# Reordering half-size sums, softmax additions and norm statistics on the vector engine, and splitting one output projection, in a two-layer attention kernel

## The chip, the cores and the metric

The kernel runs on one core of a Trainium2 chip. The metric is the device time of one execution in microseconds (us), lower being better. Engines are named as in the profile: PE (TensorE, with PEld for its weight loads), DVE (VectorE), ACT (ScalarE), POOL (GpSimd) and SP (SyncE, which here issues DMAs). "L633" is line 633 of the kernel before the change, unless the changed kernel is named.

## The reference

Eight images of 32 x 32 positions and 512 channels (1024 tokens each) pass through two attention layers, each with a group norm in front and a residual around it. All is float32.

```python
x = x + conv0(gn(x), w_qkv, w_proj, b_proj)      # gn: 32 groups, no scale or shift
x = x + conv1(gn(x), Wq, Wk, Wv, Wo, pos_emb_w, pos_emb_h)

def conv0(x, ...):                               # 16 heads of 32
    q, k, v = split_heads(x.reshape(B, 1024, 512) @ w_qkv)
    attn = softmax(q * 32 ** -0.5 @ k.T)
    return merge_heads(attn @ v) @ w_proj + b_proj

def conv1(x, ...):                               # 4 heads of 128
    q, k, v = x @ Wq * 128 ** -0.5, x @ Wk, x @ Wv
    scores = q @ k.T + relative_logits(q, pos_emb_w, pos_emb_h)
    return merge_heads(softmax(scores) @ v) @ Wo
```

## The kernel before, in words

**Projections.** Every 512 x 512 projection of 1024 tokens is done as two units (`u`), each with seven half-size products instead of eight, a Strassen-Winograd scheme. `seven` (L397) issues the products in the order 0, 5, 1, 4, 6, 2, 3 (`ORDER`). Products 0 and 1 read quarters of the input as they are. Products 4, 5, 6 and 2 read half-size sums, which `forming` (L339, additions L360, 128 x 1024 each) makes on DVE, in this order: s1 for product 4, s2 for product 5, a difference for product 6 and s4 for product 2. A product is a chain of matmuls L327 into one PSUM bank called x, y or z. Product 5 goes into y; then `a = y + p1` (L411) is formed on DVE, and product 4 continues in the same bank y, so that it cannot start before L411 has read y. `b = y + p1` (L419) does the same after product 4, and product 2 waits for it. The tile names carry the projection: `a_wo` belongs to the output projection of layer 1 (`after_1`), `y_wp` to that of layer 0 (`after_0`).

**Output projections.** Their results are added to the residual: on POOL (L502) from copies in SBUF, on DVE (L507, with bias L509) from PSUM. In layer 1 finished parts are transposed on DVE (L947) and stored through SP's queue. In layer 0 the statistics of the second norm are taken from the finished parts (`bn_stats` L259, `bn_aggr` L260).

**Norms.** `group_norm` takes averages on a 128 x 32 tile (`turned` L285 to `var` L296, eight small DVE instructions), a power on POOL (`rstd` L300), and then four scalings on DVE (L304, 128 x 1024 each).

**Layer-0 attention.** `attention_0` treats 4 heads at a time, in 64 steps per image (4 head groups, 2 halves of queries, 8 blocks of keys). A step makes a score tile `ps` (16 matmuls L603, 4 PSUM banks, one buffer), its exponential `e` (ACT L611, two buffers in SBUF), its share of the output `acc` (8 matmuls L622), and adds `e` to the running sum `es` on DVE (L631 for the first pair, L633 for the other six). After eight steps the sum goes through PE (`sums` L643) and is normalised on DVE and POOL. So the next `ps` waits for `e` to have read the last one, and `e` waits until DVE has added the `e` of two steps before.

**Passes and order.** The main loop runs nine passes. In pass b, layer-0 attention of image b is laid beside other work (`side_by_side`), in this order: output projection of layer 0 of image b-1 (`after_0`), output projection of layer 1 of image b-2 (`after_1`) woven with the second norm of image b-1 (`norm_1`), the three projections of layer 1 (`second`), attention of layer 1, and the first projections of image b+1 (`before_0`). The order on each engine is fixed when the kernel is built: by priorities that follow program order, and by `tc.issue_after(ins)`, which holds an instruction behind another in its engine's order. The variables `begun`, `half_done` and `added` hold the last L411, L419 and layer-1 addition for that purpose. Weights are streamed from HBM by SP, one 128 KB chunk to a product, in the order of a written `plan`.

In pass 1 `after_0` makes its four sums from layer-0's output before its products; in later passes the sums are made ahead, by a hook in the last projection (`forms_0`). After the last pass, `after_last` does the output projection of the last image with its products in two parts: `two_first` (0 and 1 of both units) and then `five_last`.

Of the kernel before, what the change touches and what calls it, by code (L numbers as in the profile page):

```python
# [27 lines left out]
def quick_path(  # L28
# [23 lines left out]
    nc = tc.nc  # L52
# [267 lines left out]

    added = [None]
# [17 lines left out]
    def forming(x, name, room=None, behind=None):  # L339


        a11, a12 = x[:, :HC, :NB], x[:, HC:, :NB]
        a21, a22 = x[:, :HC, NB:], x[:, HC:, NB:]
        if room is not None:
            s1, s2, s4 = [room[:, i, :].rearrange("p (c n) -> p c n", n=NB) for i in range(3)]
        else:
            s1, s2, s4 = [
                mem.tile([P, HC, NB], F32, tag=f"form{i}", name=f"f{i}_{name}", bufs=1)
                for i in (1, 2, 4)
            ]  # L350
        for op, out, one, other in (
            (nc.vector.tensor_add, s1, a21, a22),
            (nc.vector.tensor_sub, s2, s1, a11),
            (nc.vector.tensor_sub, a21, a11, a21),
            (nc.vector.tensor_sub, s4, a12, s2),
        ):

            late = behind() if behind is not None else None
            with tc.issue_after(late.ins) if late is not None else nullcontext():
                last_form[0] = op(out, one, other)  # L360
            yield 0
        return [a11, a12, s4, a22, s1, s2, a21]
# [34 lines left out]
    def seven(fs, u, rows, sink, name, hook=None):  # L397
# [13 lines left out]
        begun[0] = nc.vector.tensor_add(a, y, p1)  # L411
# [7 lines left out]
        half_done[0] = nc.vector.tensor_add(b, y, p1)  # L419
# [17 lines left out]
    def two_first(fs, u, sink, name):  # L437

        product = taken(fs, u, False)
        x = bank(f"x_{name}")  # L440
        product(x, 0, True)
        p1 = snapshot("e1", f"p1_{name}")
        nc.scalar.copy(p1, x)
        product(x, 1, False)
        sink.c11(x)
        return p1

    def five_last(fs, u, sink, name, p1):
        product = taken(fs, u, False)
        y = bank(f"y_{name}")  # L450
        product(y, 5, True)
        a = snapshot("es1", f"a_{name}")
        nc.vector.tensor_add(a, y, p1)
        sink.early(p1, a)
        product(y, 4, False)
        b = snapshot("es1", f"b_{name}")
        nc.vector.tensor_add(b, y, p1)
        sink.middle(b)
        z = bank(f"z_{name}")
        product(z, 6, True)  # L460
        p7 = snapshot("e1", f"p7_{name}")
        nc.scalar.copy(p7, z)
        product(y, 2, False)
        sink.c12(y, p1)
        product(z, 3, False)
        sink.c21(z, a)
        sink.c22(b, p7)

# [121 lines left out]
    def attention_0(q, k, v, b, blocks=range(NT)):  # L590
# [23 lines left out]
        def back(m, h, j, e):  # L614
# [14 lines left out]
            if j == blocks[1]:  # L629
                state["esum"] = mem.tile([P, HB, NB], F32, tag="es0", name=f"es_{name}", bufs=1)  # L630
                nc.vector.tensor_add(state["esum"], state["first"], e)  # L631
            elif j != blocks[0]:
                nc.vector.tensor_add(state["esum"], state["esum"], e)  # L633
# [153 lines left out]
    def load(b, st):  # L787
# [21 lines left out]
        st["xn"] = yield from forming(x, f"xn0_{b}", behind=lambda: added[0])  # L809
# [66 lines left out]
    def before_0(b, st, hook=None):  # L876
# [4 lines left out]
        yield from project_T(fs, WQ0, st["q"], f"q0_{b}")  # L881
# [9 lines left out]
    def after_0(b, st, hook=None):  # L891

        fs = st.pop("ao0") if "ao0" in st else forms(st["q0"], f"ao0_{b}", block(f"forms_{b}"))
        x = st["x1"] = block(f"x1T_{b}")
        xT = fetch(st["kept"], x)
        for u in range(2):
            bias = [bproj_sb[:, n * HC + u : n * HC + u + 1] for n in range(2)]
            stream.unit(WP, False, u)
            yield from seven(
                fs, u, False, Onto(halves(xT, u), bias), f"wp_{b}_{u}", hook if u else None  # L900
            )
            for n in range(2):
                statistics(st, xT, n * HC + u, f"1_{b}")

    def norm_1(b, st, after=None, behind=None):
        xT = chunks(st["x1"])
        st["kept"] = put_away(xT, f"1_{b}")
        yield from group_norm(st, xT, f"1_{b}", after, behind)

    def second(b, st):  # L910

        fs = forms(st.pop("x1"), f"xn1_{b}")
        q = st["ao"] = block(f"q1_{b}")
        yield from project_T(fs, WQ1, chunks(q), f"q1_{b}")
# [53 lines left out]
    def after_last(b, st):  # L968
# [4 lines left out]
        early = [x[:, :HC, :NB], x[:, HC:, :NB]]  # L973
        p1s = []
        for u in range(2):
            stream.unit(WO, False, u)
            p1s.append(two_first(early, u, sinks[u], f"wo_{b}_{u}"))
        fs = forms(x, f"ao1_{b}")
        for u in range(2):
            stream.unit(WO, False, u)  # L980
            five_last(fs, u, sinks[u], f"wo_{b}_{u}", p1s[u])
# [32 lines left out]

    def marked():
# [17 lines left out]

    FIRST = units(WQ0) + units(WK0) + units(WV0, True)
    plan = [(m, m is WV0, u, ORDER) for u in range(2) for m in (WV0, WQ0, WK0)]
    for b in range(B + 1):
        if b >= 1:
            plan += units(WP)
# [8 lines left out]
    plan += [(WO, False, u, some) for some in (FIRST_TWO, LAST_FIVE) for u in range(2)]  # L1047
# [24 lines left out]
    for b in range(B + 1):  # L1072
# [11 lines left out]
        if last is not None:  # L1084
            if past is not None:
                norm = norm_1(b - 1, last, after=lambda: half_done[0])
# [4 lines left out]
            if past is not None:  # L1091
                rest.append(woven(later(after_1, b - 2, past), norm, 3, 3))
# [22 lines left out]
        else:  # L1115
            rest.append(woven(rest_of_first(here), incoming, 0, 2))
# [505 lines left out]
```

## Time and profile before

| | us |
|---|---|
| median of 3 runs | 3848.02 (3847.01 to 3848.98) |
| profiled execution, its own time | 3848.35 |
| span of the profiled execution | 3846.6 |
| PE busy | 3789.4 (99%) |
| DVE busy | 2555.1 (66%) |
| ACT busy | 1760.2 (46%) |
| POOL busy | 621.6 (16%) |

The profile is of one execution. Busy time is the time in which an engine has an instruction at work; the rest of the span is its idle time, and a number in square brackets at an instruction in a timeline is the engine's idle time just before it, with what ended it. The granted clock (PEclk) is the share of full speed that TensorE was given, 0.998 as a mean over this execution. The profiled time is 0.33 us over the median, and 1.75 us over its span.

### The profile page before, as it was taken

To read this page: it belongs to the slowest core of one execution; us is meant where nothing else is said; L and a number is where in the kernel's file an instruction comes from. 1 tells how busy PE (TensorE), PEld (TensorE's weight loads), DVE (VectorE), ACT (ScalarE), POOL (GpSimd) and SP (SyncE) were. 2 spreads that over 40 slices of the span, in tenths; PEclk is the share of its full clock that TensorE was granted. 3 is DMA by queue.
4 is the path that set the end of the run, shared out by engine and by line. 5 is a ranking of instruction groups with operands and counts; after the bars stand their busy time and mean duration, and the time that the engine had idled before them with its cause. 6 is when DMAs were issued, how large, how long until landed. Compare 5 with 4: busy or idle time off the path is not lost.

```text
span 3846.6 us, 79883 instructions
## 1 busy us (share of the span) xinstructions
PE 3789.4 (99%) x34478; PEld 1376.3 (36%) x34478; DVE 2555.1 (66%) x2966; ACT 1760.2 (46%) x1830; POOL 621.6 (16%) x398
## 2 busy tenths in 40 slices
PE   9999999999999999999999999999999999999998
PEld 4222244222443234432343323433234332334353
DVE  6777775686755866558665686656866568665544
ACT  3554544545444454444544445444454445553132
POOL 1342101121011211012101121111210112001201
PEclk9999999999999999999999999999999999999999
DMA  6122120142202322023120241103311023110321
GB/s 185 61 88 81 41 59 6 44 122 62 56 9 83 89 54 56 13 92 85 45 55 16 93 93 38 50 21 98 90 40 41 26 96 78 33 37 31 109 41 26
DMA packets 482983, 234.72 MB, mean 61 GB/s; under 512 B 269600, under 2 KB 461376, under 8 KB 481600
## 3 DMA queue, kind: packets, MB, share of 16 engines
q1 hardware_dynamic: 470992, 213.74, 20.5%
q0 software_dynamic: 2608, 13.70, 1.0%
q8 instruction: 273, 4.47, 0.5%
q10 hardware_dynamic: 9024, 2.10, 0.3%
q14 instruction: 86, 0.70, 0.1%
HBM read 170.72 MB, written 58.72 MB: 60 GB/s over the span
## 4 chain that ended last, share of the span: by engine, by line
PE 88%; DVE 7%; ACT 2%; issue 2%; DMA 0%; SPq 0%; POOL 0%; DVEq 0%; ACTq 0%; POOLq 0%
PE ps L603 12%; PE ps L718 11%; PE acc L730 11%; PE acc L622 11%; PE y_q L327 4%; PE y_v L327 4%; PE y_k L327 4%; PE ps L719 3%; PE x_q L327 3%; PE x_v L327 3%; PE z_k L327 3%; PE x_k L327 3%; PE z_q L327 3%; PE z_v L327 3%; DVE es L633 2%; ACT e L611 2%
## 5 line engine op out<-in xcount | busy, mean ns | idle before, releaser
L611 ACT ACTIVATE e<-ps 128x2048 f32<-128x2048 f32 x512 | 961.7, 1878 | 840.1 <-PE ps L603 630.0
L633 DVE TENSOR_TENSOR es<-es,e 128x2048 f32<-128x2048 f32 x384 | 894.8, 2330 | 403.7 <-ACT e L611 400.4
L603 PE MATMUL ps<-q,k 32*64 32x512 f32 x8192 | 579.1, 614 | 17.1 <-ACT e L611 17.1
L622 PE MATMUL acc<-e,v 128*32 128x512 f32 x4096 | 546.7, 605 | 0.0
L721 ACT ACTIVATE e<-ps 128x512 f32<-128x512 f32 x512 | 305.7, 597 | 507.1 <-PE ps L719 436.4
L718 PE MATMUL ps<-q,k 128*128 128x512 f32 x1024 | 525.0, 594 | 0.2 <-DVE posT L704 0.2
L730 PE MATMUL acc<-e,v 128*128 128x512 f32 x1024 | 522.0, 593 | 0.3 <-ACT e L721 0.3
L588 POOL TENSOR_TENSOR q<-q,su 128x512 f32<-128x512 f32 x128 | 212.7, 1662 | 1550.3 <-DVE su L584 1427.7
L741 DVE TENSOR_TENSOR es<-es,e 128x512 f32<-128x512 f32 x384 | 290.4, 756 | 251.0 <-ACT e L721 248.4
L719 PE MATMUL ps<-posT,sel 128*128 128x512 f32 x512 | 406.6, 794 | 0.0
L718 PEld LDWEIGHTS ps<-q,k 128*128 128x128 f32 x1024 | 192.5, 190 | 230.1 <-issue 218.5
L603 PEld LDWEIGHTS ps<-q,k 32*64 32x64 f32 x8192 | 120.6, 130 | 410.1 <-issue 223.5
L730 PEld LDWEIGHTS acc<-e,v 128*128 128x128 f32 x1024 | 193.1, 189 | 147.3 <-issue 92.6
L622 PEld LDWEIGHTS acc<-e,v 128*32 128x32 f32 x4096 | 81.3, 108 | 412.7 <-issue 366.1
L631 DVE TENSOR_TENSOR es<-e,e 128x2048 f32<-128x2048 f32 x64 | 171.6, 2681 | 32.8 <-ACT e L611 32.7
L568 DVE STREAM_TRANSPOSE tu<-su 128x512 f32<-128x512 f32 x128 | 90.5, 707 | 97.3 <-ACT su L566 95.7
L719 PEld LDWEIGHTS ps<-posT,sel 128*128 128x128 f32 x512 | 97.3, 190 | 122.5 <-issue 122.5
L566 ACT COPY su<-sums 128x512 f32<-128x512 f32 x128 | 74.9, 585 | 131.2 <-PE sums L643 81.5
L704 DVE TENSOR_TENSOR posT<-pp,posT 32x512 fp32r<-32x512 f32 x128 | 112.0, 875 | 31.9 <-ACT posT L699 30.6
L492 POOL TENSOR_TENSOR k<-b_k,p_k 128x512 f32<-128x512 f32 x32 | 52.0, 1624 | 483.4 <-ACT p_k L425 472.7
L699 ACT CAST posT<-pp 32x512 fp32r<-32x512 f32 x128 | 105.9, 827 | 45.8 <-PE pp L686 44.7
L492 POOL TENSOR_TENSOR v<-b_v,p_v 128x512 f32<-128x512 f32 x32 | 51.6, 1614 | 433.9 <-ACT p_v L425 433.9
(214 smaller groups left out, 4546.0 us busy)
## 6 DMA issues: line engine op xcount, KB each, us to landing
w_qkv<-ws_qkv SPq DMA_DIRECT2D x168, 128.0 KB, 2.5
d<-x0T SPq DMA_DIRECT2D x32, 512.0 KB, 3.0
x1T<-d SPq DMA_DIRECT2D x32, 512.0 KB, 5.9
d<-x1T SPq DMA_DIRECT2D x32, 512.0 KB, 3.6
x2T<-d SPq DMA_DIRECT2D x32, 512.0 KB, 6.1
w_qkv<-in_L_conv_w_qkv SPq DMA_DIRECT2D x126, 128.0 KB, 2.2
out<-ot SPq DMA_DIRECT2D x240, 64.0 KB, 2.0
xs<-in_x SPq DMA_DIRECT2D x224, 64.0 KB, 2.5
```

The source lines that it names most:

```text
L327: ins = nc.tensor.matmul(out[columns, :], weights[:, columns], moving, start=start, stop=stop, skip_group_check=open_sum,)
L588: nc.gpsimd.tensor_tensor(dst, dst, su, op=ALU.mult)
L603: nc.tensor.matmul(ps[some, r, :], k[m][rows, j * P + 64 * i : j * P + 64 * i + 64], q[m][rows, h * NB : (h + 1) * NB], start=True, stop=True,
L611: nc.scalar.activation(e, ps, AF.Exp, scale=D0 ** -0.5)
L622: nc.tensor.matmul(acc[r * D0 : (r + 1) * D0, :], v[:, j, c0 : c0 + D0], e[:, r, :], start=(j == blocks[0]), stop=(j == blocks[-1]),)
L631: nc.vector.tensor_add(state["esum"], state["first"], e)
L633: nc.vector.tensor_add(state["esum"], state["esum"], e)
L718: nc.tensor.matmul(ps, k[h][:, keys], q[:, h, queries], start=True, stop=False)
L719: nc.tensor.matmul(ps, sel_flat[:, keys], posT[:, h, queries], start=False, stop=True)
L721: nc.scalar.activation(e, ps, AF.Exp, scale=1.0 / math.sqrt(D1))
L730: nc.tensor.matmul(acc, v[:, j, h * D1 : (h + 1) * D1], e, start=(j == 0), stop=(j == NT - 1),)
L741: added[0] = nc.vector.tensor_add(state["esum"], state["esum"], e)
```

## The change

Four things change, all of them in the order of instructions; the instructions themselves and the bytes moved stay the same.

- **Sums of a norm in two parts.** In the passes 2 to 6 (`sums_1`) the first two sums for layer 1's first projection are made at the end of the norm, each behind the latest layer-0 addition; the third and fourth come later, between products of that projection. For image 1 (`before_0` in pass 0) the fourth sum comes between products of its first projection.
- **Additions behind readers.** While the norm runs beside layer 1's output projection (`with_norm`), each layer-0 addition (L631, L633) is held behind the latest L411 or L419 (`reader`). The four scalings L304 are held behind the latest such addition (`summed`), and are woven in at other places (gap 14 at the places 0, 3, 6, 8 and 9 instead of gap 3). On DVE this gives, in the passes 2 to 6: `a_wo` of the first unit ahead of the addition that stood before it, the third L633 ahead of the scalings, the scalings in two pairs with an addition between them, `a_wo` and `b_wo` of the second unit each ahead of an addition. In pass 7 the order changes likewise, with other steps.
- **First output projection in two parts.** In pass 1 `after_0` goes through the new `in_two_parts`: products 0 and 1 of both units first, with the four sums beside them, then the five others. `after_last` uses the same function. The weights are streamed in that order.
- **Last statistics.** In pass 8 the last statistics (`look`) come behind the L411 of layer 1's output projection.

```diff
@@ -320,2 +320,6 @@
+    reader = [None]
+    summed = [None]
+    beside_norm = [False]
+
     added = [None]
@@ -338,3 +342,3 @@
-    def forming(x, name, room=None, behind=None):
+    def forming(x, name, room=None, behind=None, into=None):
@@ -350,3 +354,6 @@
             ]
-        for op, out, one, other in (
+        fs = [a11, a12, s4, a22, s1, s2, a21]
+        if into is not None:
+            into.extend(fs)
+        for i, (op, out, one, other) in enumerate((
             (nc.vector.tensor_add, s1, a21, a22),
@@ -355,5 +362,7 @@
             (nc.vector.tensor_sub, s4, a12, s2),
-        ):
+        )):
-            late = behind() if behind is not None else None
+            late = None
+            if behind is not None:
+                late = behind[i]() if isinstance(behind, tuple) else behind()
             with tc.issue_after(late.ins) if late is not None else nullcontext():
@@ -361,3 +370,3 @@
             yield 0
-        return [a11, a12, s4, a22, s1, s2, a21]
+        return fs
@@ -410,3 +419,3 @@
         a = snapshot("es1", f"a_{name}")
-        begun[0] = nc.vector.tensor_add(a, y, p1)
+        reader[0] = begun[0] = nc.vector.tensor_add(a, y, p1)
         sink.early(p1, a)
@@ -418,3 +427,3 @@
         b = snapshot("es1", f"b_{name}")
-        half_done[0] = nc.vector.tensor_add(b, y, p1)
+        reader[0] = half_done[0] = nc.vector.tensor_add(b, y, p1)
         sink.middle(b)
@@ -443,4 +452,6 @@
         nc.scalar.copy(p1, x)
+        yield HC
         product(x, 1, False)
         sink.c11(x)
+        yield HC
         return p1
@@ -452,8 +463,10 @@
         a = snapshot("es1", f"a_{name}")
-        nc.vector.tensor_add(a, y, p1)
+        begun[0] = nc.vector.tensor_add(a, y, p1)
         sink.early(p1, a)
+        yield HC
         product(y, 4, False)
         b = snapshot("es1", f"b_{name}")
-        nc.vector.tensor_add(b, y, p1)
+        half_done[0] = nc.vector.tensor_add(b, y, p1)
         sink.middle(b)
+        yield HC
         z = bank(f"z_{name}")
@@ -462,4 +475,6 @@
         nc.scalar.copy(p7, z)
+        yield HC
         product(y, 2, False)
         sink.c12(y, p1)
+        yield HC
         product(z, 3, False)
@@ -467,2 +482,22 @@
         sink.c22(b, p7)
+        yield HC
+
+    def in_two_parts(x, m, sinks, name, room=None, done=lambda u: None, behind=None):
+
+        early = [x[:, :HC, :NB], x[:, HC:, :NB]]
+        p1s, fs = [], []
+
+        def products():
+            for u in range(2):
+                stream.unit(m, False, u)
+                p1s.append((yield from two_first(early, u, sinks[u], f"{name}_{u}")))
+
+        def sums():
+            fs.extend((yield from forming(x, name, room, behind)))
+
+        yield from woven(products(), sums(), 0, 1)
+        for u in range(2):
+            stream.unit(m, False, u)
+            yield from five_last(fs, u, sinks[u], f"{name}_{u}", p1s[u])
+            done(u)
@@ -630,5 +665,9 @@
                 state["esum"] = mem.tile([P, HB, NB], F32, tag="es0", name=f"es_{name}", bufs=1)
-                nc.vector.tensor_add(state["esum"], state["first"], e)
+                other = state["first"]
             elif j != blocks[0]:
-                nc.vector.tensor_add(state["esum"], state["esum"], e)
+                other = state["esum"]
+            if j != blocks[0]:
+
+                with tc.issue_after(reader[0].ins) if beside_norm[0] else nullcontext():
+                    summed[0] = nc.vector.tensor_add(state["esum"], other, e)
             if j != blocks[-1]:
@@ -808,3 +847,12 @@
         yield from group_norm(st, xT, f"0_{b}")
-        st["xn"] = yield from forming(x, f"xn0_{b}", behind=lambda: added[0])
+        if b > 1:
+            st["xn"] = yield from forming(x, f"xn0_{b}", behind=lambda: added[0])
+            return
+        fs = st["xn"] = []
+        done, read = lambda: summed[0], lambda: half_done[0]
+        sums = st["sums0"] = forming(x, f"xn0_{b}", behind=(done, read, read, done), into=fs)
+        yield next(sums)
+        yield 0
+        for _ in range(2):
+            yield next(sums)
@@ -880,3 +928,5 @@
         st["q"] = chunks(st["q0"])
-        yield from project_T(fs, WQ0, st["q"], f"q0_{b}")
+        yield from woven(
+            project_T(fs, WQ0, st["q"], f"q0_{b}"), st.pop("sums0", iter(())), 0, 2 * len(ORDER)
+        )
         st["k"] = chunks(block(f"k0_{b}"))
@@ -892,13 +942,29 @@
-        fs = st.pop("ao0") if "ao0" in st else forms(st["q0"], f"ao0_{b}", block(f"forms_{b}"))
         x = st["x1"] = block(f"x1T_{b}")
         xT = fetch(st["kept"], x)
+        sinks = [
+            Onto(halves(xT, u), [bproj_sb[:, n * HC + u : n * HC + u + 1] for n in range(2)])
+            for u in range(2)
+        ]
+
+        def done(u):
+            def look(u=u):
+                for n in range(2):
+                    statistics(st, xT, n * HC + u, f"1_{b}")
+
+            if b == B - 1 and u:
+                st["look"] = look
+            else:
+                look()
+
+        if "ao0" not in st:
+            yield from in_two_parts(
+                st["q0"], WP, sinks, f"wp_{b}", block(f"forms_{b}"), done, lambda: summed[0]
+            )
+            return
+        fs = st.pop("ao0")
         for u in range(2):
-            bias = [bproj_sb[:, n * HC + u : n * HC + u + 1] for n in range(2)]
             stream.unit(WP, False, u)
-            yield from seven(
-                fs, u, False, Onto(halves(xT, u), bias), f"wp_{b}_{u}", hook if u else None
-            )
-            for n in range(2):
-                statistics(st, xT, n * HC + u, f"1_{b}")
+            yield from seven(fs, u, False, sinks[u], f"wp_{b}_{u}", hook if u else None)
+            done(u)
@@ -906,2 +972,6 @@
         xT = chunks(st["x1"])
+        if "look" in st:
+
+            with tc.issue_after(begun[0].ins):
+                st.pop("look")()
         st["kept"] = put_away(xT, f"1_{b}")
@@ -909,7 +979,20 @@
+    def sums_1(b, st):
+
+        fs = st["xn1"] = []
+        done = lambda: summed[0]
+        sums = st["sums1"] = forming(
+            st.pop("x1"), f"xn1_{b}", behind=(done, done, done, lambda: half_done[0]), into=fs
+        )
+        for _ in range(2):
+            yield next(sums)
+
     def second(b, st):
-        fs = forms(st.pop("x1"), f"xn1_{b}")
+        if "xn1" in st:
+            fs, sums = st.pop("xn1"), st.pop("sums1")
+        else:
+            fs, sums = forms(st.pop("x1"), f"xn1_{b}"), iter(())
         q = st["ao"] = block(f"q1_{b}")
-        yield from project_T(fs, WQ1, chunks(q), f"q1_{b}")
+        yield from woven(project_T(fs, WQ1, chunks(q), f"q1_{b}"), sums, 0, 2 * len(ORDER), (0, 3))
         posT = block(f"posT_{b}", dtype=F32R)
@@ -972,11 +1055,3 @@
         sinks = [Onto(halves(xT, u), then=put_out(b, st, xT, u)) for u in range(2)]
-        early = [x[:, :HC, :NB], x[:, HC:, :NB]]
-        p1s = []
-        for u in range(2):
-            stream.unit(WO, False, u)
-            p1s.append(two_first(early, u, sinks[u], f"wo_{b}_{u}"))
-        fs = forms(x, f"ao1_{b}")
-        for u in range(2):
-            stream.unit(WO, False, u)
-            five_last(fs, u, sinks[u], f"wo_{b}_{u}", p1s[u])
+        run(in_two_parts(x, WO, sinks, f"wo_{b}"))
@@ -1014,2 +1089,7 @@
+    def with_norm(part):
+        beside_norm[0] = True
+        yield from part
+        beside_norm[0] = False
+
     def marked():
@@ -1033,2 +1113,5 @@
+    def in_parts(m):
+        return [(m, False, u, some) for some in (FIRST_TWO, LAST_FIVE) for u in range(2)]
+
     FIRST = units(WQ0) + units(WK0) + units(WV0, True)
@@ -1037,3 +1120,3 @@
         if b >= 1:
-            plan += units(WP)
+            plan += units(WP) if b > 1 else in_parts(WP)
         if b == 1:
@@ -1046,3 +1129,3 @@
             plan += FIRST if b else units(WQ0) + units(WK0)[:1] + units(WV0, True)
-    plan += [(WO, False, u, some) for some in (FIRST_TWO, LAST_FIVE) for u in range(2)]
+    plan += in_parts(WO)
@@ -1085,3 +1168,7 @@
             if past is not None:
-                norm = norm_1(b - 1, last, after=lambda: half_done[0])
+                norm = norm_1(
+                    b - 1, last, after=lambda: half_done[0], behind=lambda: summed[0]
+                )
+                if coming is not None:
+                    norm = chain(norm, later(sums_1, b - 1, last))
             else:
@@ -1091,3 +1178,3 @@
             if past is not None:
-                rest.append(woven(later(after_1, b - 2, past), norm, 3, 3))
+                rest.append(with_norm(woven(later(after_1, b - 2, past), norm, 3, 14, (0, 3, 6, 8, 9))))
                 total += PRODUCT
@@ -1115,3 +1202,3 @@
         else:
-            rest.append(woven(rest_of_first(here), incoming, 0, 2))
+            rest.append(woven(rest_of_first(here), incoming, 0, 1))
             total += PRODUCT
```

## The prediction

> **What bounds the kernel now.** I read the page's busy line first, then the waits of PE, then the timeline around each wait. Times below are us from the span's start in the profiled execution.
>
> ```profile
> PE 3789.4 (99%) x34478; PEld 1376.3 (36%) x34478; DVE 2555.1 (66%) x2966; ACT 1760.2 (46%) x1830; POOL 621.6 (16%) x398
> ```
>
> PE is busy for 3789.4 of 3846.6, so it bounds the kernel, and the change leaves its instructions alone. What can be gained is its idle time, 57.2, and time lost at a reduced clock. The largest lines of PE's waits (total, times, longest):
>
> ```profile
> PE ps L603 <- ACT e L611: 17.1, 16, 2.9
> PE y_wo L327 <- DVE a_wo L411: 9.1, 6, 1.8
> PE sums L643 <- DVE es L633: 3.1, 2, 1.8
> PE y_wp L327 <- DVE forms L360: 2.5, 1, 2.5
> ```
>
> They are short and many. ACT is only 46% busy, so a wait for ACT's `e` usually means that ACT was itself held up. The timeline of pass 2, at the norm beside layer 1's output projection, shows by what:
>
> ```profile
> 843.11 2.98 DVE L304 TENSOR_SCALAR x1T<-x1T,back,rstd 128x1024 f32<-128x1024 f32 x4 [1.20 <-POOL rstd L300]
> 846.01 2.29 DVE L633 TENSOR_TENSOR es<-es,e 128x2048 f32<-128x2048 f32 x1
> 848.38 1.88 ACT L611 ACTIVATE e<-ps 128x2048 f32<-128x2048 f32 x1 [5.25 <-DVE es L633]
> 850.32 1.12 PE L603 MATMUL ps<-q,k 32*64 32x512 f32 x16 [0.98 <-ACT e L611]
> ...
> 854.02 4.64 DVE L633 TENSOR_TENSOR es<-es,e 128x2048 f32<-128x2048 f32 x2
> 858.59 0.68 DVE L411 TENSOR_TENSOR a_wo<-y_wo,p_wo 128x512 f32<-128x512 f32 x1
> 859.32 1.92 PE L327 MATMUL y_wo<-f_ao,w_o 128*32 128x512 f32 x16 [1.42 <-DVE a_wo L411]
> ```
>
> Two stalls, both by DVE's order. The addition at 846.01 stands behind four scalings, ACT's `e` waits for it (848.38), and PE for ACT: 0.98. Later `a_wo` stands behind two additions, and PE waits 1.42 to go on in the bank `y_wo`. The same pair recurs in passes 3 to 6 with the same figures, except 1.77 for the second in pass 4. DVE is idle for 1.20 just before the scalings: it lacks order there, not capacity.
>
> **The change part by part.**
>
> *Passes 2 to 6.* With the new order I replayed DVE, ACT and PE by the durations above. The third addition comes behind `var` (L296, done at 841.92): it needs an `e` that was done at 839.44, so it runs from 841.9 to 844.2. ACT's next `e` then waits only for its `ps` (matmuls at 845.51 to 846.62) and is done at 848.6; PE wants it at 849.34, behind 16 matmuls of x_wo. The 0.98 goes, with 0.7 to spare. `a_wo` of the second unit, ahead of its addition, is done near 855.4; PE wants y_wo at 856.7. So 1.42 goes, with 1.3 to spare. Gain: 5 x 0.98 + 4 x 1.42 + 1.77 = 12.35.
> What stands behind the moved work: the first addition (L631) now waits behind `a_wo` of the first unit, which waits for PE's y_wo (done 830.9). L631 runs from 831.8 to 834.0 instead of 831.1 to 833.35; `e` behind it ends at 836.0, and PE's next `ps` is due at 836.28: 0.3 to spare, the thinnest place of the change. The second pair of scalings and the two later sums are off the path: I place the fourth sum at 881.7, and product 2 of the next projection wants it at 885.5. Without that cover a late sum would cost 1.2 to 2.3 (L360 at 1.22 to 2.29 in this trace) per pass. SP gets one store a place earlier (`out` of the first part); its loads keep their order there, and POOL's order is unchanged.
>
> A rule speaks against putting the addition there. The Trainium skill, "GPSIMD Engine Reference", section 1 (Specifications), says that GpSimd's SBUF interfaces are shared with VectorE and that it contends with DVE instructions that have two SBUF inputs. The moved L633 is one, and POOL's `rstd` (1.02 at 842.06), which now runs with DVE idle, falls beside it. The trace agrees on contention: POOL's L502 took 3.34 beside an addition at 835.70, 1.28 alone at 839.17. By the rows as they stand, `rstd` is done at 843.1, and the first scalings start behind the addition, at 844.2. Stretched by 3.34/1.28, `rstd` ends at 844.7. The scalings' first pair (1.5) and the addition behind it then end near 848.6 instead of 848.1, and `e` wants that only after 850.4. By both the sum is 12.35; the rule takes only slack.
>
> *First output projection, pass 1.*
>
> ```profile
> 322.96 1.07 PE L603 MATMUL ps<-q,k 32*64 32x512 f32 x2 [1.04 <-ACT e L611]
> ...
> 325.25 1.23 DVE L360 TENSOR_TENSOR forms<-forms,q 128x1024 f32<-128x1024 f32 x1
> 326.53 2.94 PE L327 MATMUL y_wp<-forms,w_p 128*32 128x512 f32 x16 [2.50 <-DVE forms L360]
> 329.40 1.72 PE L603 MATMUL ps<-q,k 32*64 32x512 f32 x14
> ...
> core 0: us, PE busy (x) PEld busy (x) DVE busy (x) ACT busy (x) POOL busy (x), PEclk, DMA share, GB/s
> 325.00:330.00 5.00, 3.47 (x23) 0.83 (x30) 4.19 (x5) 0.00 (x0) 0.00 (x0) 0.73 0.91 362
> ```
>
> Product 5 waits 2.50 for the second sum, and then the granted clock is 0.73 over 325 to 330: 16 matmuls took 2.94 where 1.90 is usual (340.28), and 14 of L603 1.72 where 16 take 1.11. That is 1.04 + 0.61 = 1.65 more. With products 0 and 1 of both units first, 32 matmuls that need no sum fill the gap, and the 1.04 at 322.96 lies under them too: 1.04 + 2.50 + 1.65 = 5.2. Against it: L631 now stands behind three sums and so holds ACT's third `e`; by replay that stalls `ps` for about 0.9 in all. Net 4.3. Here a rule gives another figure. The Trainium skill, "TensorE: Matmul & The Clock Gate", section "Why this matters for your kernels", asks for no idle gaps over about 3 us, one idle window bringing the half clock. By it the 2.50 would not have cost the clock: 5.2 - 1.65 = 3.55, net 2.65. The trace differs: a gap of 2.50 here and one of 1.82 before 165.60 (clock 0.69 over 165 to 170) were each followed by it, one of 2.92 before 141.17 was not. I go by the row, 4.3; ends 2.6 and 5.2.
> POOL's additions and SP's weight chunks are reordered only here; no chunk is wanted before it was, in its new place, and the chunks land 2.2 to 2.5 after issue. A late one would show as PE waiting for DMA; I take 0, with up to 2.5 in the range.
>
> *Fourth sum of image 1, pass 0.*
>
> ```profile
> 134.94 2.00 DVE L360 TENSOR_TENSOR f_xn<-x0T,f_xn 128x1024 f32<-128x1024 f32 x1
> 136.87 2.28 DVE L631 TENSOR_TENSOR es<-e,e 128x2048 f32<-128x2048 f32 x1
> 139.24 1.88 ACT L611 ACTIVATE e<-ps 128x2048 f32<-128x2048 f32 x1 [5.47 <-DVE es L631]
> 141.17 1.12 PE L603 MATMUL ps<-q,k 32*64 32x512 f32 x16 [2.92 <-ACT e L611]
> ```
>
> The sum leaves its place before L631, which then starts 1.95 earlier: 1.95 of the 2.92 goes. The sum comes back two additions later, where DVE has 1.32 idle before 148.05; product 2 wants it near 155. If it pushes the slow additions at 156.08 (9.38 for two, beside POOL's L152), the stall of 1.82 there grows, at worst taking the 1.95 back. I take 1.95; ends 0 and 5.4 (1.95 + 1.82 + 1.65, should that stall and its clock go too).
>
> *Last statistics, pass 8.* `a_wo` at 3575.18 stood behind three L259 and an L260, and PE waited 1.62 for it, to 3575.90. With the statistics behind it, I take 1.4; ends 0.8 and 1.62.
>
> *Pass 7.* A wait of 1.31 (sums behind an addition, 3214.35) goes, but `a_wo` ahead of L631 there holds the next `e`: about 0.9 is lost again. Net 0.4; ends -1 and 1.3. *After the last pass* the order of PE and DVE is the same: 0.
>
> Sum: 12.35 + 4.3 + 1.95 + 1.4 + 0.4 = 20.4, so 3848.35 - 20.4 = 3827.95 against the profiled execution; the median is 0.33 lower. I say 3828. Stalls at 239.98 (1.53), 376.1 (1.85), 269.8 (1.14) and at the start (8.3 with the wait for x) stay, their order being unchanged.
>
> **The rivals.**
> *Waits move on (3836).* Additions held behind L411 and L419 make `e` late one step further on. For it: the 0.3 to spare at 836.28, and DVE is 82% busy in this stretch (4.89 of 6.00 over 842 to 848). Against it: the other spare times are 0.7 to 1.8. If one stall as large as the first, 0.98, plus 0.6 at the thin place, comes back in each of the five passes, 5 x 1.6 = 8 of the 20.4 is lost.
> *Only the single places gain (3840.7).* The scheduler's order holds but DVE's instructions stretch beside POOL (L633 2.54 at 835.36 against 2.29), and the loop keeps its stalls: 12.35 and the 0.4 drop out, 7.65 stays: 3848.35 - 7.65 = 3840.7.
> *Slower (3869).* One mechanism: at the thin place, L631 behind `a_wo` of the first unit. If L631 is more than 0.3 late, PE stalls there for the rest; from about 1.8 the half clock follows, as before 165.60, and the price is 1.8 + 1.65 = 3.45. At both units of six passes that is 12 x 3.45 = 41.4, against a gain of 20.4: 21 slower. It decides from 2.35 per place (28.2 in all: the gain and 7.7 more). The stall of 1.8 needs y_wo, and so L631, 2.1 later than by the replay. Nothing in the trace shows that.
> *It does not do what it says.* Were the orders as before where the stalls are, 3848. The order of the built kernel is as described, so this is small.
>
> **How the numbers follow.** Forecast as worked out, 3823 to 3833: 0.62. Waits move on, 3833 to 3840: 0.22. Only single places, 3840 to 3845: 0.07. No change: 0.04. Slower: 0.03. Better than 3823, with the stall of 165.60 and its clock gone: 0.02. The range 3822 to 3840 holds the first two and some of the last, 0.85; it is wider than the first case since the spare times are thin. Faster by over 0.2% (7.7, about what a measurement of this kernel tells from no change) means below 3840.3: 0.88; within 0.2%: 0.09; slower: 0.03.
>
> **What would show it.** In the profile after, PE's wait for `a_wo` L411 should fall from 9.1 to about 1, that for `forms` from 2.5 to near 0, and that for `e` from 17.1 to about 11. DVE's busy time should stay within a few us of 2555. The clock should be 1.00 at 325 to 330. The forecast is wrong if the waits for `e` keep or exceed 17, or a new line stands in the waits of PE: for the sums L360, for DMA of `w_p`, or for L419.

## The result, and the profile after

The changed kernel takes 3832.17 us (median of 6 runs, 3830.98 to 3833.13) against 3847.34 for the kernel before (median of 6, 3846.50 to 3848.98): 15.2 us less, ratio 0.996 with a 95% interval of 0.9947 to 0.9973. The profiled execution took 3830.98 (span 3829.2), 17.4 less than the one before.

The page's busy line of the changed kernel:

```profile
PE 3786.5 (99%) x34478; PEld 1377.4 (36%) x34478; DVE 2562.9 (67%) x2966; ACT 1761.1 (46%) x1830; POOL 653.4 (17%) x398
```

PE was busy for 2.9 less and the span is 17.4 shorter, so 14.5 of it is idle time of PE that went (57.2 to 42.7). The 2.9 less of busy time, with the same number of matmuls, is mostly time at the half clock: the profile before had two stretches with a granted clock of 0.5 (3.41 each, from 166.87 and from 327.30) between its start and its end, the one after had none. POOL is busy for 32 more with the same 398 instructions, since the additions that are held now run beside them (622.8 again in no_held below, where they are not held); the last section comes back to it.

The waits of PE after (total, times, longest). L420 is L411 of before, L428 is L419, L646 is L611, L672 is L631 and L633, L638 is L603; L464 is `a` in `five_last`:

```profile
PE ps L638 <- ACT e L646: 13.4, 16, 1.8
PE y_wp L331 <- DVE a_wp L464: 2.6, 2, 1.8
PE y_wo L331 <- DVE a_wo L420: 0.7, 1, 0.7
PE y_k L331 <- DVE b_k L428: 0.4, 1, 0.4
```

The wait for `a_wo` fell from 9.1 to 0.7, and the waits for `forms` (2.5) and for `es` (3.1) are off the list. The wait for `e` fell from 17.1 to 13.4 only, and there are new ones: `y_wp` for `a_wp`, and a small one, `y_k` for `b_k`. A wait for L419 was one of the forecast's signs of being wrong. The timeline of pass 2 shows what became of the loop's two stalls:

```profile
825.68 1.28 POOL L623 TENSOR_TENSOR q<-q,su 128x512 f32<-128x512 f32 x1 [11.55 <-DVE su L619]
826.03 3.07 DVE L672 TENSOR_TENSOR es<-e,e 128x2048 f32<-128x2048 f32 x1
...
829.22 1.88 ACT L646 ACTIVATE e<-ps 128x2048 f32<-128x2048 f32 x1 [5.05 <-DVE es L672]
...
831.15 1.12 PE L638 MATMUL ps<-q,k 32*64 32x512 f32 x16 [0.44 <-ACT e L646]
...
836.28 2.28 DVE L672 TENSOR_TENSOR es<-es,e 128x2048 f32<-128x2048 f32 x1
836.81 2.63 POOL L300 TENSOR_TENSOR rstd<-var,neg_half 128x4 f32<-128x4 f32 x1 [1.85 <-DVE var L296]
...
839.48 1.53 DVE L304 TENSOR_SCALAR x1T<-x1T,back,rstd 128x1024 f32<-128x1024 f32 x2 [0.31 <-POOL rstd L300]
...
849.75 0.68 DVE L420 TENSOR_TENSOR a_wo<-y_wo,p_wo 128x512 f32<-128x512 f32 x1
...
851.54 1.90 PE L331 MATMUL y_wo<-f_ao,w_o 128*32 128x512 f32 x16
```

The addition at 836.28 now stands ahead of the scalings, which come in pairs; `a_wo` at 849.75 is done 1.1 before PE takes y_wo up again at 851.54, with no wait in brackets. Both old stalls are gone. A small one is left at 831.15: the first addition, behind `a_wo`, took 3.07. It starts while POOL's instruction of 825.68 is at work; in the kernel before it started 0.22 ahead of the same instruction, and took 2.25 while POOL took 3.17:

```profile
831.10 2.25 DVE L631 TENSOR_TENSOR es<-e,e 128x2048 f32<-128x2048 f32 x1
831.32 3.17 POOL L588 TENSOR_TENSOR q<-q,su 128x512 f32<-128x512 f32 x1 [11.55 <-DVE su L584]
```

Where the 17.4 came from, by the start of the same exponential in both traces (the gain at the end of a stretch less that at its begin):

| stretch | forecast | in the profiles |
|---|---|---|
| pass 0, the sums of image 1 | 1.95 | 3.97 |
| pass 1, the first output projection | 4.3 | 1.75 |
| passes 2 to 6, five norms | 12.35 | 11.16 |
| pass 7 | 0.4 | 0.03 |
| pass 8 and the end | 1.4 | 0.5 |

### The profile page after: what moved, and what is told of

Same layout as the page of the kernel before. It is cut to its first block, busy times and chain, and to the rows that moved or that the text cites. A ratio compares the mean times of both kernels' runs of the same rounds, so it can differ in the third digit from the quotient of the medians.

```text
span 3829.2 us, 79905 instructions
## 1 busy us (share of the span) xinstructions
PE 3786.5 (99%) x34478; PEld 1377.4 (36%) x34478; DVE 2562.9 (67%) x2966; ACT 1761.1 (46%) x1830; POOL 653.4 (17%) x398
## 4 chain that ended last, share of the span: by engine, by line
PE 91%; DVE 5%; ACT 2%; issue 1%; DMA 0%; POOL 0%; DVEq 0%; SPq 0%; ACTq 0%; POOLq 0%
PE ps L638 13%; PE acc L657 12%; PE ps L757 11%; PE acc L769 11%; PE y_q L331 4%; PE y_v L331 4%; PE y_k L331 4%; PE ps L758 3%; PE x_q L331 3%; PE x_v L331 3%; PE z_k L331 3%; PE z_q L331 3%; PE x_k L331 3%; PE z_v L331 3%; DVE es L672 2%; ACT e L646 2%
## 5 line engine op out<-in xcount | busy, mean ns | idle before, releaser
L646 ACT ACTIVATE e<-ps 128x2048 f32<-128x2048 f32 x512 | 961.8, 1879 | 821.3 <-PE ps L638 637.9
L672 DVE TENSOR_TENSOR es<-es,e 128x2048 f32<-128x2048 f32 x384 | 890.8, 2320 | 386.6 <-ACT e L646 384.1
L638 PE MATMUL ps<-q,k 32*64 32x512 f32 x8192 | 577.8, 613 | 13.4 <-ACT e L646 13.4
L623 POOL TENSOR_TENSOR q<-q,su 128x512 f32<-128x512 f32 x128 | 201.7, 1575 | 1527.5 <-DVE su L619 1402.6
L638 PEld LDWEIGHTS ps<-q,k 32*64 32x64 f32 x8192 | 120.4, 129 | 405.5 <-issue 212.7
L672 DVE TENSOR_TENSOR es<-e,e 128x2048 f32<-128x2048 f32 x64 | 176.5, 2758 | 31.4 <-ACT e L646 31.3
L603 DVE STREAM_TRANSPOSE tu<-su 128x512 f32<-128x512 f32 x128 | 90.6, 708 | 97.3 <-ACT su L601 95.7
```

The source lines that it names most:

```text
L623: nc.gpsimd.tensor_tensor(dst, dst, su, op=ALU.mult)
L638: nc.tensor.matmul(ps[some, r, :], k[m][rows, j * P + 64 * i : j * P + 64 * i + 64], q[m][rows, h * NB : (h + 1) * NB], start=True, stop=True,
L646: nc.scalar.activation(e, ps, AF.Exp, scale=D0 ** -0.5)
L672: summed[0] = nc.vector.tensor_add(state["esum"], other, e)
```

## The experiments

All but the last are edits of the changed kernel; "slower" and "faster" are against its 3832.17 unless said otherwise. The changed kernel was not timed again beside them. The kernel before was, and its medians were 3847.34 to 3847.84, so that a difference of less than about 1 us says little.

**The loop's part undone (no_loop).**

```diff
-                norm = norm_1(b - 1, last, after=lambda: half_done[0], behind=lambda: summed[0])
-                if coming is not None:
-                    norm = chain(norm, later(sums_1, b - 1, last))
+                norm = norm_1(b - 1, last, after=lambda: half_done[0])
...
-                rest.append(with_norm(woven(later(after_1, b - 2, past), norm, 3, 14, (0, 3, 6, 8, 9))))
+                rest.append(woven(later(after_1, b - 2, past), norm, 3, 3))
```

> The changed kernel without its part in the passes 2 to 7: additions not held behind readers, scalings not spread, all four sums of layer 1's norm made at once. Theory (three separate gains, the loop's the largest): the pair of stalls (0.98 and 1.42) is back in each of the passes 2 to 6, 11.2 us are lost, 3832.2 + 11.2 = 3843.4; PE's wait for a_wo L420 is 9 us again. Rival (the loop's stalls matter little and most of the gain comes from the half-clock windows that went): under 3836.

Measured: 3843.18, which is 11.0 slower (forecast by the first theory 11.2). Its waits of PE:

```profile
PE ps L638 <- ACT e L646: 15.4, 16, 1.9
PE y_wo L331 <- DVE a_wo L420: 7.8, 6, 1.4
```

The pair of stalls is back in all five passes (0.92 to 1.28 for `e`, 1.42 for `a_wo`), and pass 7's wait for the sum (1.31) is back in place of its 1.39 for `e`. Its profiled execution, 11.5 slower than the changed kernel's, had no half clock between start and end either, so the clock is no part of the difference of the profiles: the loop's order is worth 11 of the 15.

**One half of it at a time.** First the additions are no longer held behind readers (no_held):

```diff
-        beside_norm[0] = True
+        beside_norm[0] = False
         yield from part
```

> The changed kernel without holding any addition behind a reader; scalings and sums stay as in the change. Theory (holding additions cures the wait for a_wo, the scalings' place cures the wait for e): a_wo of the second unit stands behind one addition, 1.3 of stall comes back in five passes, while the 0.44 goes: 5 x 0.9 = 4.5 slower than the changed kernel, 3836.5; no wait for e after the scalings. Rival (the split of the scalings alone does it all): 3830, faster than the changed kernel by 5 x 0.44.

Measured: 3836.91, 4.7 slower (expected 4.5). The timeline of pass 2:

```profile
849.58 2.28 DVE L672 TENSOR_TENSOR es<-es,e 128x2048 f32<-128x2048 f32 x1
851.78 0.68 DVE L420 TENSOR_TENSOR a_wo<-y_wo,p_wo 128x512 f32<-128x512 f32 x1
852.51 1.92 PE L331 MATMUL y_wo<-f_ao,w_o 128*32 128x512 f32 x16 [1.38 <-DVE a_wo L420]
```

One addition ahead of `a_wo` is enough to cost 1.38, in each of five passes. The 0.98 did not come back, and the 0.44 was gone. So the two measures are separate: the hold cures the wait for `a_wo`, the place of the scalings the wait for `e`.

Then the scalings are let go instead (no_scal):

```diff
-                    b - 1, last, after=lambda: half_done[0], behind=lambda: summed[0]
+                    b - 1, last, after=lambda: half_done[0]
...
-                rest.append(with_norm(woven(later(after_1, b - 2, past), norm, 3, 14, (0, 3, 6, 8, 9))))
+                rest.append(with_norm(woven(later(after_1, b - 2, past), norm, 3, 3)))
```

> The changed kernel without the scalings held behind additions and with the old weaving (gap 3): the order that results has two scalings ahead of the third addition and two behind it. Theory (it is the four in a row, 2.98 and a wait for rstd of 1.20, that made e late; two in front leave the addition done at about 841.2, before ps needs e): no loss over 0.3 a pass, 3832 to 3833.5. Rival (the addition must stand first): 0.98 is back in five passes, 3837.

Measured: 3839.55, 7.4 slower: neither figure. The first theory was right on its wait: with two scalings ahead of it the third addition ends in time, and the 0.98 is not back. But the old weaving also moves the norm's later work, and the second sum with it:

```profile
866.02 0.68 DVE L542 TENSOR_TENSOR x2T<-z_wo,x2T 128x512 f32<-128x512 f32 x1
866.62 1.71 DVE L369 TENSOR_TENSOR f_xn<-f_xn,x1T 128x1024 f32<-128x1024 f32 x1
868.38 1.92 PE L331 MATMUL y_q<-f_xn,w_q 128*32 128x512 f32 x16 [0.56 <-DVE f_xn L369]
```

In the changed kernel that sum runs at 859.01, 8 us before product 5 wants it; here it stands behind an addition to the residual that waits for PE, and PE waits 0.56 for it. With 0.25 for `y_wo` at 846.58 that is about 0.9 a pass. Pass 7 lost 3.6 more in the profile: a stall of 1.93 and a stretch of half clock after it. So the early sums are a part of their own in the change, and cost when they slip.

**The first output projection in seven products again (no_two).**

```diff
-            yield from in_two_parts(
-                st["q0"], WP, sinks, f"wp_{b}", block(f"forms_{b}"), done, lambda: summed[0]
-            )
-            return
-        fs = st.pop("ao0")
+            fs = forms(st["q0"], f"ao0_{b}", block(f"forms_{b}"))
+        else:
+            fs = st.pop("ao0")
...
-            plan += units(WP) if b > 1 else in_parts(WP)
+            plan += units(WP)
```

> The changed kernel with the first output projection as before, in seven products and not in two parts. Theory (the two parts removed 5.2 us of stalls and half clock and brought 3.4 of new stalls): 1.75 slower than the changed kernel, 3834; y_wp waits 2.5 for the second sum. Rival (the forecast's own 4.3 is right and the new stalls come from somewhere else): 3836.5. If the half clock does not come back with the stall, the first theory's figure is 3832.3.

Measured: 3833.93, 1.8 slower, the first theory's figure. Its own wait for `forms` was 3.0, and the old 1.04 was back. Its profiled execution was the slowest of five (3835.09), with two stretches of half clock at this place, and lost 3.0 here; how many the other four had is not known. The two parts remove the stalls, and put the wait for `a_wp` (2.6) and 0.83 for `ps` in its place. The timeline of the changed kernel shows how:

```profile
328.66 2.29 DVE L672 TENSOR_TENSOR es<-es,e 128x2048 f32<-128x2048 f32 x1 [0.21 <-ACT e L646]
...
330.87 0.68 DVE L464 TENSOR_TENSOR a_wp<-y_wp,p_wp 128x512 f32<-128x512 f32 x1
...
331.60 1.92 PE L331 MATMUL y_wp<-forms,w_p 128*32 128x512 f32 x16 [0.81 <-DVE a_wp L464]
...
346.39 2.24 DVE L672 TENSOR_TENSOR es<-es,e 128x2048 f32<-128x2048 f32 x1
...
348.55 0.68 DVE L464 TENSOR_TENSOR a_wp<-y_wp,p_wp 128x512 f32<-128x512 f32 x1
349.29 1.92 PE L331 MATMUL y_wp<-forms,w_p 128*32 128x512 f32 x16 [1.76 <-DVE a_wp L464]
```

Both times `a_wp` stands behind one addition: the fault that the change cures in the loop, made anew here.

**That fault cured (wp_held).** The later products of the first output projection hold additions too:

```diff
     def five_last(fs, u, sink, name, p1):
...
-        begun[0] = nc.vector.tensor_add(a, y, p1)
+        reader[0] = begun[0] = nc.vector.tensor_add(a, y, p1)
...
-        half_done[0] = nc.vector.tensor_add(b, y, p1)
+        reader[0] = half_done[0] = nc.vector.tensor_add(b, y, p1)
...
             stream.unit(m, False, u)
+            beside_norm[0] = room is not None
             yield from five_last(fs, u, sinks[u], f"{name}_{u}", p1s[u])
+            beside_norm[0] = False
             done(u)
```

> The changed kernel, and in the five later products of the first output projection each layer-0 addition held behind the latest a or b (L464, L469) too. Theory (the two stalls of 0.81 and 1.76 there are the loop's second stall once more: a_wp behind an addition): both go, 2.6 faster, 3829.6. Rival (the additions, once held, make e late): the wait moves to ps, 3831.5 to 3833.

Measured: 3828.65, 3.5 faster (expected 2.6). The timeline at the same two places:

```profile
328.72 0.68 DVE L464 TENSOR_TENSOR a_wp<-y_wp,p_wp 128x512 f32<-128x512 f32 x1
...
330.96 1.90 PE L331 MATMUL y_wp<-forms,w_p 128*32 128x512 f32 x16
...
347.03 1.92 PE L331 MATMUL y_wp<-forms,w_p 128*32 128x512 f32 x16 [0.19 <-DVE a_wp L464]
```

The 0.81 is gone, 0.19 is left of the 1.76, and no wait for `ps` took their place. Between the same exponentials of the two profiles this place gains 2.6, as expected. The other 0.9 between the medians is near the scatter; fewer stretches of half clock may be a part of it, since half of the changed kernel's timed runs had a mean clock of 0.998 and four of the five here 0.999.

**The thin place (both).** wp_held, and the first unit's `a` no longer sets `reader`, so that the first addition comes ahead of it again:

```diff
-        reader[0] = begun[0] = nc.vector.tensor_add(a, y, p1)
+        begun[0] = nc.vector.tensor_add(a, y, p1)
+        if u:
+            reader[0] = begun[0]
```

> The kernel wp_held, and in the passes 2 to 7 the first addition no longer held behind a_wo of the first unit (reader is set by the first unit's b, and by the second unit's a and b). Theory (the 0.44 left in each of the passes 2 to 6 comes from L631's place behind a_wo): these stalls go, 5 x 0.44 = 2.2 faster than wp_held, 3826.4. Rival (that addition is late because it shares with POOL: it took 3.07 where 2.25 is usual): no change, 3828.6.

Measured: 3827.27 (3827.17 to 3827.96), 1.4 faster than wp_held; ratio to the kernel before 0.9946, interval 0.9933 to 0.996. The timeline of pass 2:

```profile
822.84 2.25 DVE L676 TENSOR_TENSOR es<-e,e 128x2048 f32<-128x2048 f32 x1
823.06 3.18 POOL L627 TENSOR_TENSOR q<-q,su 128x512 f32<-128x512 f32 x1 [11.54 <-DVE su L623]
...
828.02 1.11 PE L642 MATMUL ps<-q,k 32*64 32x512 f32 x16
```

The five stalls of 0.44 are gone; some 0.1 a pass comes back further on. This fits both theories in part: the place in the order decides, and it does so through POOL. The addition now starts 0.22 ahead of POOL's instruction, takes 2.25, and POOL takes 3.18; in the changed kernel it started 0.35 behind, took 3.07, and POOL took 1.28.

**The third sum behind the addition (gap2).** The kernel both, and in `in_two_parts` the sums at every second product:

```diff
-        yield from woven(products(), sums(), 0, 1)
+        yield from woven(products(), sums(), 0, 2)
```

> The kernel both, and in the first output projection the four sums woven at every second product instead of every one: on DVE the third sum comes behind the first addition (L631) and not ahead of it. Theory (that sum, 1.21, is what made e and then ps late by 0.84 near 328): the 0.84 goes, 3826.4. Rival (L631 waits for its e anyway): no change, 3827.3.

Measured: 3827.64 (3826.42 to 3829.20), not to be told from the kernel both. In its trace `ps` at 328.29 has no wait, so the 0.84 went as expected; the span is the same 3825.9, its first exponential having started 0.55 later. The stall is shown, the gain in time is not.

**The sums of image 1 where they were (no_late).** Besides the place of the fourth sum, this gives the first three their old holds back:

```diff
-        if b > 1:
+        if True:
             st["xn"] = yield from forming(x, f"xn0_{b}", behind=lambda: added[0])
             return
...
-            rest.append(woven(rest_of_first(here), incoming, 0, 1))
+            rest.append(woven(rest_of_first(here), incoming, 0, 2))
```

> The changed kernel with all four sums of image 1's first norm made at once, as before, in pass 0. Theory (the sum ahead of the addition is the cause of the stall of 2.92, and all that follows, the stall of 1.82 and its half clock, hangs on it): 4.0 slower, 3836.2. Rival (the second stall and the clock hang on how POOL's weight sums fall beside two additions, which other shifts can change): about 2, 3834.2, with no half clock near 165.

Measured: 3835.05 (3833.16 to 3836.96), 2.9 slower, between the two. The stall of 2.92 is back:

```profile
136.96 2.00 DVE L369 TENSOR_TENSOR f_xn<-x0T,f_xn 128x1024 f32<-128x1024 f32 x1
138.88 2.28 DVE L672 TENSOR_TENSOR es<-e,e 128x2048 f32<-128x2048 f32 x1
...
143.19 1.12 PE L638 MATMUL ps<-q,k 32*64 32x512 f32 x16 [2.92 <-ACT e L646]
```

In the changed kernel 0.70 is left of it, 2.2 less. But the change made a new stall just ahead, once more by an order on DVE. The first sum now comes ahead of `b_k`, an addition goes between them, and product 2 of the k projection waits. The changed kernel, then the kernel before:

```profile
125.39 1.23 DVE L369 TENSOR_TENSOR f_xn<-x0T 128x1024 f32<-128x1024 f32 x1 [1.36 <-PE y_k L331]
...
126.53 2.28 DVE L672 TENSOR_TENSOR es<-es,e 128x2048 f32<-128x2048 f32 x1
...
128.73 0.68 DVE L428 TENSOR_TENSOR b_k<-y_k,p_k 128x512 f32<-128x512 f32 x1
...
129.47 1.47 PE L331 MATMUL y_k<-f_xn,prep_qkv 128*32 128x512 f32 x9 [0.38 <-DVE b_k L428]
...
140.45 1.12 PE L638 MATMUL ps<-q,k 32*64 32x512 f32 x16 [0.70 <-ACT e L646]
```

```profile
125.31 0.69 DVE L419 TENSOR_TENSOR b_k<-y_k,p_k 128x512 f32<-128x512 f32 x1 [1.36 <-PE y_k L327]
125.92 1.22 DVE L360 TENSOR_TENSOR f_xn<-x0T 128x1024 f32<-128x1024 f32 x1
```

Between the same two exponentials around both places the changed kernel takes 14.39 (127.34 to 141.73), the kernel before 15.18 (127.27 to 142.45) and no_late 15.19: the net gain of the sums is 0.8, since PE is idle for 1.8 less but busy for 1.0 more with the same matmuls. The rest of what no_late loses in its profile (3836.85, its second slowest of six) is half clock, in stretches from 144.32 and 376.42 and a longer one at the start. The stall of 1.82 near 165 is not back, so it does not hang on the sum.

Undone singly, the loop, the first projection and the sums of image 1 cost 11.0, 1.8 and 2.9, together 15.7, about the whole 15.2. The place of the last statistics was not undone by itself.

**The kernel before, a second time (before_again).**

> The kernel before, unchanged, profiled a second time, to see what of its stalls is the same in every execution. Theory (the stalls by DVE's order are fixed; those beside POOL's weight sums, and the half clock, depend on how two free-running things fall): 2.92 near 141, 0.98 and 1.42 in the passes 2 to 6 and 2.50 near 326 again; the 1.82 near 165 and the half-clock windows can be elsewhere or missing. Rival (all are fixed by the program): the 1.82 and both half-clock windows again at the same places.

It took 3848.54, with 2.93 near 141, 2.50 near 325, and 0.98 and 1.42 in the passes (1.77 in pass 4) again. The stall near 165 was missing. First the second execution, then the first, DVE and POOL:

```profile
154.53 7.26 POOL L152 TENSOR_TENSOR prep_q<-prep_q 128x512 f32<-128x512 f32 x3
157.97 2.68 DVE L633 TENSOR_TENSOR es<-es,e 128x2048 f32<-128x2048 f32 x1
161.23 2.71 DVE L633 TENSOR_TENSOR es<-es,e 128x2048 f32<-128x2048 f32 x1 [0.58 <-ACT e L611]
```

```profile
155.63 0.58 POOL L154 DMA_DIRECT2D ws_p<-prep_p  x1
156.08 9.38 DVE L633 TENSOR_TENSOR es<-es,e 128x2048 f32<-128x2048 f32 x2
156.23 3.76 POOL L152 TENSOR_TENSOR prep_q<-prep_q 128x512 f32<-128x512 f32 x3
...
165.60 1.07 PE L643 MATMUL sums<-es,ones 128*32 128x512 f32 x8 [1.82 <-DVE es L633]
```

The same instructions of the same program: once POOL is slow and DVE nearly at full speed, once the reverse, and only then does PE stall. The half clock moved as well. By stretch, in the second execution (PEclk is third from the right):

```profile
core 0: us, PE busy (x) PEld busy (x) DVE busy (x) ACT busy (x) POOL busy (x), PEclk, DMA share, GB/s
142.00:146.00 4.00, 4.00 (x36) 1.01 (x24) 3.08 (x2) 1.88 (x1) 4.00 (x2) 0.57 0.48 185
166.00:170.00 4.00, 4.00 (x48) 0.91 (x40) 2.28 (x6) 2.46 (x2) 0.71 (x1) 1.00 0.14 37
323.00:327.00 4.00, 1.83 (x12) 0.52 (x16) 3.97 (x4) 0.00 (x0) 0.00 (x0) 0.55 0.98 374
```

In the first execution the same three stretches read 1.00, 0.61 and 1.00, and the half clock of the projection came at 327 to 331 (0.57).

## Why the prediction was right

The forecast was 3828, 20 us less; measured were 15.2 less between medians, 17.4 between the profiled executions. Step by step:

- **The two stalls of the loop** went as the replay had it, at 11.2 in the profiles and 11.0 when undone, of 12.35 forecast. The third addition ahead of the scalings and `a_wo` ahead of its addition do it separately, as no_held shows. At the thin place the forecast gave 0.3 to spare, and PE waits 0.44, 2.2 in five passes. The term that was off is the addition's duration, taken as 2.25 and measured as 3.07: the replay had the start right, but put the addition behind the start of POOL's instruction without counting that it then waits for it. Another 1.0 came unforeseen: with the stalls PE's busy time fell too, by 0.2 a norm (in pass 2, between the same exponentials, from 433.61 to 433.42 for the same 3788 matmuls).
- **The rule on the shared interfaces** (the Trainium skill, "GPSIMD Engine Reference", section 1, Specifications) held where the forecast weighed it: `rstd` took 2.63 beside the addition (estimate 2.66 from the stretch of L502), ended at 839.44, and the scalings started at 839.48. It cost only slack there. It was not applied to the addition at the thin place, where it mattered.
- **The first output projection** is the step that failed: 4.3 forecast, 1.75 found. The forecast counted the new stall of `ps` and did not follow `a_wp` behind the additions in the later products. It foresaw 0.9 of new stalls; there were 3.4 (0.83, 0.81, 1.76). wp_held shows that this was an order that could be had better.
- **The clock.** The row was right that gaps under the 3 us of the rule (the Trainium skill, "TensorE: Matmul & The Clock Gate", section "Why this matters for your kernels") can bring the half clock: 2.50 did in both executions of the kernel before (in the second together with the 1.04 ahead of it), 1.82 in the first. But one row of one execution was read as fixed: the place moves between executions. Counting 1.65 for one stretch in pass 1 and none in pass 0 was a guess about one draw.
- **The sums of image 1** gave 0.8, not 1.95. The stall that the forecast looked at shrank by 2.2, but the first three sums had moved as well, which it put at nothing, and the first of them made `b_k` late. The other 3.2 of the 3.97 is the stall near 165 and its clock, which the kernel before lost in its first profiled execution and not in its second; the forecast had it only in an end of its range. That pass 0 gained more than forecast is luck.
- **The statistics of pass 8:** the 1.62 went, and 0.47 and 0.69 came behind the next residual addition and the scalings; 0.5 is left of 1.4. **Pass 7:** the wait of 1.31 went, and 1.39 came for `e` at 3205.94, behind `a_wo`, where the forecast had 0.9. Neither was tested by a run of its own.
- **The rivals.** Waits that move on were real, at one place a pass and 0.44 instead of 1.6, in the projection, and in pass 0. The slower one did not occur: the thin place was late by 0.44, far from 1.8.

That 15.2 is less than 17.4 has to do with the clock too. The timed runs of the changed kernel fall in two groups: 3831.0 to 3831.5 with a mean clock of 0.999 and 3832.8 to 3833.1 with 0.998, 1.7 apart, as one stretch of half clock would make. The profiled execution is of the first. So the total came near by errors of both signs: the loop and the projection gave less than forecast, and the stall near 165, not counted on, made up for a part of it.

## What to carry to other kernels

When the engine that bounds a kernel waits for an engine that is itself far from full, look at the order on that engine: what the bounding engine wants soon goes ahead of what only keeps buffers free, and both ahead of work that is wanted late. After moving work, replay to the end of the stretch that the move reorders, since the same fault can come up a few instructions on (here behind `a_wp` and `b_k`), and where a spare time is thin, look at which of DVE and POOL starts first there. Split a difference of two profiles into what recurs in every execution and what is one draw of clock and contention; a second profile of the unchanged kernel tells them apart.

## What the runs showed of the hardware

- An addition on DVE with two SBUF inputs and an instruction on POOL that overlap do not share: the one that starts first keeps its time, and the other waits. In the eleven traces one addition of 128x2048 met one POOL addition of 128x512, and no other TENSOR_TENSOR of DVE, 563 times. In the 262 cases in which DVE started first it took 2.25 to 2.29 (alone 2.24 to 2.30) and POOL 1.95 to 3.39; in the 301 in which POOL started first it took 1.26 to 1.30 (alone 1.26 to 1.29) and DVE up to 3.35. So the thin place of pass 2 could have been forecast from the two starts.
- One of the 4928 additions of these traces took longer than one such wait makes it (3.45 at most): the first of the two at 156.08, with 6.08. It started ahead of POOL's additions and all the same waited for three of them, while a DMA issue of POOL (155.63 to 156.21) was under way. Why is open. PE's 1.82 at 165.60 is its wait for the second of the two.
- The half clock comes in stretches of 3.41 us (142.50 to 145.91, and 323.41 to 330.24 for two of them in the second execution of before). Within an execution they start a whole number of 3.413 apart: 166.87 and 327.30 in the first are 47 steps apart, 144.32 and 376.42 in no_late 68. Where this grid lies differs between executions.
- How a stall falls on that grid decides most cases. Cut into such windows, and without the start, the eleven traces have five windows at full clock with 1.93 or more of PE idle; each was followed by half clock. Of eleven with 1.76 to 1.86 idle three were, and of those with less, 1.63 at most, none. So the stall of 2.92 near 141 did nothing in the first execution, where it lay across two windows, and brought the half clock in the second, where 2.28 of it fell into one (two rows of the first execution, one of the second, columns as above):

```profile
136.15:139.56 3.41, 2.10 (x20) 0.39 (x12) 3.41 (x3) 0.32 (x1) 1.25 (x2) 1.00 0.59 167
139.56:142.98 3.42, 1.81 (x24) 0.53 (x28) 2.02 (x2) 2.09 (x2) 1.33 (x1) 1.00 0.97 345
...
139.09:142.50 3.41, 1.13 (x20) 0.32 (x24) 2.01 (x3) 1.88 (x1) 0.52 (x1) 1.00 0.98 359
```

The stall of 1.85 in pass 1, of the same size in every kernel here, is at the edge: whole in one window it was followed by half clock in no_late (0.57 over 376 to 380) and not in the changed kernel. What decides there is open.
